# A graph convolution on one core: first nodes loaded in two parts, the last group but one multiplied tile by tile, the last group scaled from PSUM

## The chip, the cores and the metric

The kernel runs on one core of one Trainium2 chip. Its metric is the device time of one execution in microseconds; several executions are timed, and the median is compared. The core's engines are TensorE (PE in the profile, with its weight loads as PEld), VectorE (DVE), ScalarE (ACT), GpSimd (POOL) and SyncE (SP), which only issues DMAs here.

## The reference

One equivariant graph convolution with a residual and a layer norm over 12,500 nodes of 128 features and 412,500 edges, which come sorted by destination node:

```python
f0 = x0 @ W1_0e / sqrt(32);  f1 = einsum('nui,uw->nwi', x1, W1_1o) / sqrt(32)
feat, self = halves of f0, f1
h   = gelu(gelu(edge_attr_8 @ W_mlp1 / sqrt(8)) @ W_mlp2 / sqrt(64))
w00, w01, w10, w11 = h @ Wp_00, h @ Wp_01, h @ Wp_10, h @ Wp_11      # per edge
e0, e1 = feat0[src], feat1[src];  ea0, ea1 = edge_attr_4[:, :1], edge_attr_4[:, 1:]
mid0 = concat(w00*e0*ea0, w11*sum(e1*ea1)/sqrt(3))
mid1 = concat(w01*e0*ea1, w10*e1*ea0)
n0, n1 = segment_sum(mid0, dst), segment_sum(mid1, dst)
y = cos(pi/8)*self + sin(pi/8)*(n0 @ W2_0e, einsum(n1, W2_1o))
out = layernorm(x + y)            # over the 128 features of a node
```

## The kernel before

**Tiling.** Nodes go in 25 groups of 512 (four tiles of 128; the last group, 24, has one full tile and one of 84). Edges go in 806 runs of 512 (four tiles of 128), four runs to a chunk, 202 chunks. Destination nodes are sorted, so a chunk's edges reach a window of at most 96 nodes from the chunk's first node (`first_at`), and each tile's edges a narrower window from the tile's own first node (`tile_first`, shown as `tf` in the profile).

**First stage.** For each group, PE transposes the loaded rows of `x` (`turn`, L294), ACT copies them to `xT` (L295), PE multiplies by the weights (`features_of`, L301), DVE copies the product (L304) and ACT's queue stores it to a DRAM table (`store_nodes`, L260). SP's queue loads `x` six groups ahead (L252), one small load a group from the list of `weight_loads` (L925), the edge inputs of the first chunks (`load_edges`, L496), and after the groups the addresses for the main loop (`aid_load`, `aid_at` and `pick` in the profile, L959). POOL gathers rows of `x` for the first 18 runs with indirect DMAs (`gather`, L222).

**Main loop, one run at a time.** POOL gathers from the table, 18 runs ahead, into one of 19 buffers `G`. A few of a run's rows are not gathered: DVE (L190) and ACT (L192) pick columns out of `xT`, which PE multiplies (L198), and SP copies some rows singly (L209). PE and ACT compute the edge weights (`radial`, `mlp1` L536 and L540, `mlp2` L551 and L556, `weights` L569), DVE forms the messages `M` (L637, L641), PE sums them into the chunk's window (`segments`, L666 and L668; L660 clears the window), and DVE adds the window to the accumulator (`add`, L681). Before it builds a chunk's selection, DVE reads one element of each of its gathered tiles (`seen`, L597), which waits for those gathers.

**Node groups.** When a group's edges are all in (`due`), `norm` calls `moments`: PE multiplies each of its tiles by `ws` (L698) and by four blocks of `wpost` (L701) into a PSUM tile named `h`, which has two buffers that the edge weights use too; ACT copies the result to `y` (L706, L708). `statistics` (DVE, L714, L715), `deviations` (L720, L721) and `normalise` (L727 to L742) follow a chunk later, and SP stores the group. Group 23 (`before_last`) is multiplied in run 801 (chunk 200), group 24 in `norm_last` after the last run.

**Order.** Each engine's order is the order of the code. DMAs of SP's and ACT's queues share eight completion counters (`DMAHW0` to `DMAHW7`), handed out in turn; a DMA is not issued before the one that had its counter last has landed, whichever of the two queues issued that.

Of the kernel before, what the change touches and what calls it, by code (L numbers as in the profile page):

```python
# [53 lines left out]
LNB = 2  # L54
TURN_AT = (7, 9, 11, 13, 15, 17, 18, 20, 22, 24)
# [3 lines left out]
def gnn_kernel(ctx: ExitStack, tc: tile.TileContext, x, src, dst, ea4, ea8, w1_0, w1_1, wm1, wm2,  # L59
# [277 lines left out]
    def weight_loads():  # L337

        yield w1r, sub(wm1, 0, [[0, P // RAD], [HID, RAD], [1, HID]])
        yield w2b, sub(wm2, 0, [[0, 2], [HID, HID], [1, HID]])  # L340
        for j, w in enumerate((wp00, wp01, wp10, wp11)):
            yield wpb[:, j * MUL:(j + 1) * MUL], sub(w, 0, [[0, 2], [MUL, HID], [1, MUL]])
        for t, w in ((w20, w2_0), (w21, w2_1)):
            yield t[:MUL, :], w[:MUL, :]
            yield t[MUL:, :], sub(w, MUL * MUL, [[0, 3], [MUL, MUL], [1, MUL]])
        yield first_node, sub(dst, 0, [[1, 1], [CH * SB, NCH]])
        for b, t in enumerate(tile_first):
            c0, n = b * P, t.shape[0]
            last = c0 + n == NCH and E < NCH * CH * SB
            if last:  # L350
                yield (t[n - 1:n, :].rearrange("a (k o) -> a k o", o=1),
                       sub(dst, (NCH - 1) * CH * SB, [[1, 1], [0, CH * Q], [1, 1]]))
                k = -(-(E - (NCH - 1) * CH * SB) // P)
                yield t[n - 1:n, :k], sub(dst, (NCH - 1) * CH * SB, [[k * P, 1], [P, k]])
            yield t[:n - last], sub(dst, c0 * CH * SB, [[CH * SB, n - last], [P, CH * Q]])
# [52 lines left out]
    def tile_places():  # L408

        for b, t in enumerate(tile_first):  # L410
# [8 lines left out]
            nc.vector.tensor_scalar(t, off, 4.0, None, op0=OP.mult)  # L419
# [225 lines left out]
    def places(c):  # L645

        b, r = divmod(c, P)
# [37 lines left out]
    before_last = due[NCH - 1][0] - 1  # L685

    def moments(b, sums=None):
        n0, nn, full, tail, tiles = group(b)
        if not pend:
# [3 lines left out]
        j = len(pend)  # L693
        pend.append(b)
        pt = ps.tile([P, XB, P], F32, name="h")
        at = n0 - base[-1] if b in due[NCH - 1] else 0
        for t, k in tiles:
# [5 lines left out]
            else:  # L703
                nc.vector.tensor_tensor(pt[:k, t, :], pt[:k, t, :], sums[:k, t, :], op=OP.add)
        if full:
            nc.scalar.activation(Y["y"][:, j, :full, :], pt[:, :full, :], AF.Copy)  # L706
        if tail:
            nc.scalar.activation(Y["y"][:tail, j, full, :], pt[:tail, full, :], AF.Copy)  # L708

    def statistics(b):  # L710
        j = pend.index(b)
        st = wk.tile([P, XB, 6], F32, name="bst")
        for t, k in group(b)[4]:
            nc.vector.bn_stats(st[:k, t, :], Y["y"][:k, j, t, :])  # L714
# [8 lines left out]
    def normalise(last=False, keep=False):  # L723
# [9 lines left out]
        for j, b in enumerate(pend):  # L733
            if b in done:
                continue
            for t, k in group(b)[4]:
                i = j * XB + t - i0
                if last and t % 2:
                    nc.vector.tensor_scalar(y[:k, j, t, :], y[:k, j, t, :], r[:k, i:i + 1], m[:k, i:i + 1],
                                            op0=OP.mult, op1=OP.add)  # L740
                    continue
                nc.scalar.activation(y[:k, j, t, :], y[:k, j, t, :], AF.Identity,  # L742
                                     bias=m[:k, i:i + 1], scale=r[:k, i:i + 1])
            store_nodes(nc.sync, out, b, y[:, j])
# [4 lines left out]
    def norm(bs):  # L749
        for b in bs:  # L750
            moments(b)
# [14 lines left out]
    def norm_last(bs):  # L766
# [6 lines left out]
        if len(pend) > len(done):  # L773
            deviations()
            normalise(True)

# [119 lines left out]
    with tc.manual_schedule(engines={PE, ACT, DVE, SP}):  # L896
# [7 lines left out]
        for b in range(min(AHEAD, NG)):  # L904
# [9 lines left out]
                 NG // 2 + 9: tile_places, NG // 2 + 10: lambda: mlp2(1), NG // 2 + 11: make_ws, NG: make_wpost}  # L914
# [20 lines left out]
        late = list(aid_load())  # L935
# [10 lines left out]
        for s in range(NCH * CH + CH):  # L946
# [79 lines left out]
            if s == 2:  # L1026
                nc.vector.memset(owns[1], 0.0)
            if s == 5:
# [38 lines left out]
```

## Time and profile before

| | |
|---|---|
| median of 3 runs | 3556.44 us (3555.64 to 3560.35) |
| the profiled execution: its time, its span | 3556.29 us, 3554.4 us |
| PE, PEld busy | 3159.9 us (89%), 2755.6 us (78%) |
| DVE busy | 3129.2 us (88%) |
| ACT busy | 2797.6 us (79%) |
| POOL busy | 2667.6 us (75%) |
| mean granted clock of PE | 0.932 |

In rows of instructions the columns are the start in us from the span's start, the duration in us, engine, line, operation, output and inputs, count, and in brackets the idle time of the engine before it with what ended it. Rows that say SPq or ACTq are issues of DMAs. In rows of waits they are the time in total, the number, and the longest. In rows of windows they are the stretch, its length, the busy time of PE, PEld, DVE, ACT and POOL with their instructions, the granted clock, the busy share of the DMA engines and GB/s. In rows of groups they are the count, the busy time with the mean of one in ns, and the idle time before them. In rows of one tile's instructions they are the count, the shortest, median and longest duration in ns, and when the first and the last start. Rows of the chain are its pieces in order of time: start, length, what ran.

### The profile page before, as it was taken

What the parts mean: (1) busy time and instruction counts of PE and PEld (TensorE: products, weight loads), DVE (VectorE), ACT (ScalarE), POOL (GpSimd) and SP (SyncE); (2) the same over time, 40 slices, a digit from 0 to 9 for tenths busy, and PEclk for the clock granted to TensorE, in tenths of its full rate; (3) what the DMA queues carried; (4) which work ended last, traced back from release to release, by engine and by line L of the source; (5) the groups of instructions that cost most, each with busy time, mean ns of one, the idle gap of its engine ahead of it and who ended that gap; (6) DMA issues with size and microseconds to landing.
All of it is one profiled execution on the core that took longest, in us unless ns stands there. A gap on an engine that the chain in (4) does not pass through costs nothing. (4 is left out here: it accounts for less than half of the span.)

```text
span 3554.4 us, 143693 instructions
## 1 busy us (share of the span) xinstructions
PE 3159.9 (89%) x28598; PEld 2755.6 (78%) x28598; DVE 3129.2 (88%) x29317; ACT 2797.6 (79%) x23671; POOL 2667.6 (75%) x2804
## 2 busy tenths in 40 slices
PE   6899898998898988998899898898899989888888
PEld 6777777787777777877788787787787777777777
DVE  2699999999999999999899899888899888889897
ACT  3488788788888888887887888877787887788785
POOL 7777777777777777777777777777777777777775
PEclk8999999998999999899998899989899999999998
DMA  8322332223322223322323323323323232232221
GB/s 199 70 62 68 63 64 65 63 61 74 64 60 67 63 60 74 64 60 62 68 61 70 67 59 64 65 63 68 65 62 64 59 69 63 60 69 63 60 65 47
DMA packets 579225, 239.29 MB, mean 67 GB/s; under 512 B 483651, under 2 KB 528747, under 8 KB 578347
## 3 DMA queue, kind: packets, MB, share of 16 engines
q0 software_dynamic: 89536, 183.55, 20.3%
q1 hardware_dynamic: 468041, 40.02, 9.1%
q10 hardware_dynamic: 20770, 6.47, 0.8%
q8 instruction: 252, 4.13, 0.5%
q14 instruction: 626, 5.13, 0.5%
HBM read 217.00 MB, written 12.80 MB: 65 GB/s over the span
## 5 line engine op out<-in xcount | busy, mean ns | idle before, releaser
L222 POOL DMA_INDIRECT G<-table,idx x2726 | 2598.9, 953 | 836.7 <-issue 718.5
L192 ACT ACTIVATE gt<-xT 128x1 f32 x22016 | 2166.7, 190 | 73.3 <-issue 53.6
L190 DVE COPY gt<-xT 128x1 f32 x25216 | 1728.6, 144 | 212.1 <-issue 172.9
L666 PE MATMUL sums<-own,M 128*128 128x96 f32 x6446 | 1354.8, 294 | 74.3 <-DVE M L641 73.0
L668 PE MATMUL sums<-own,M 128*128 128x96 f32 x6446 | 1319.7, 288 | 85.1 <-DVE M L641 84.1
L666 PEld LDWEIGHTS sums<-own,M 128*128 128x128 f32 x6446 | 1037.5, 201 | 181.9 <-DVE M L641 101.7
L668 PEld LDWEIGHTS sums<-own,M 128*128 128x128 f32 x6446 | 1035.3, 202 | 108.9 <-DVE M L641 107.6
L641 DVE TENSOR_TENSOR M<-w,G 128x384 f32<-128x384 f32 x1612 | 880.1, 547 | 0.0
L569 PE MATMUL w<-wpb,h 64*128 64x128 f32 x6448 | 649.3, 305 | 57.8 <-DVE M L641 56.3
L569 PEld LDWEIGHTS w<-wpb,h 64*128 64x128 f32 x6448 | 496.5, 197 | 199.6 <-issue 74.3
L637 DVE TENSOR_TENSOR M<-w,G 128x256 f32<-128x256 f32 x806 | 333.4, 414 | 34.4 <-issue 19.9
L540 ACT ACTIVATE h<-h 128x512 f32<-128x512 f32 x404 | 216.3, 586 | 178.6 <-PE h L536 165.7
L536 PE MATMUL h<-eT,w1b 64*128 64x128 f32 x3232 | 288.7, 319 | 8.4 <-ACT e L523 8.3
L536 PEld LDWEIGHTS h<-eT,w1b 64*128 64x128 f32 x3232 | 241.3, 218 | 38.7 <-ACT e L523 13.7
L556 ACT ACTIVATE h<-h 128x512 f32<-128x512 f32 x404 | 213.5, 577 | 26.3 <-PE h L551 22.5
L551 PE MATMUL h<-h,w2b 64*64 64x256 f32 x3232 | 222.6, 391 | 0.0
L199 ACT ACTIVATE G<-h 128x128 f32<-128x128 f32 x369 | 96.4, 277 | 120.5 <-PE h L198 76.4
L198 PE MATMUL h<-wf,gt 128*128 128x128 f32 x738 | 143.5, 294 | 1.9 <-ACT h L556 0.9
L529 ACT ACTIVATE eT<-h 128x128 f32<-128x128 f32 x202 | 56.0, 277 | 112.7 <-PE h L527 89.5
L551 PEld LDWEIGHTS h<-h,w2b 64*64 64x64 f32 x3232 | 104.5, 133 | 44.8 <-issue 0.5
L630 DVE TENSOR_TENSOR own<-oh,e 128x512 f32<-128x512 f32 x202 | 137.6, 681 | 0.7 <-issue 0.2
L681 DVE TENSOR_TENSOR acc<-sums,acc 128x384 f32 x202 | 111.2, 550 | 9.7 <-issue 6.2
(113 smaller groups left out, 1329.1 us busy)
## 6 DMA issues: line engine op xcount, KB each, us to landing
G<-table SPq DMA_DIRECT2D x7168, 0.5 KB
G<-table,idx POOLq DMA_INDIRECT x2726
e<-in_edge_attr SPq DMA_DIRECT2D x201, 64.0 KB
own<-in_x SPq DMA_DIRECT2D x24, 256.0 KB
table<-acc ACTq DMA_DIRECT2D x24, 256.0 KB
xt<-in_edge_attr SPq DMA_DIRECT2D x24, 256.0 KB
out<-y SPq DMA_DIRECT2D x24, 256.0 KB
xt<-in_dst SPq DMA_DIRECT2D x5, 256.0 KB
```

The costliest lines, as they stand in the source:

```text
L190: nc.vector.tensor_copy(to, col)
L192: nc.scalar.activation(to, col, AF.Copy)
L222: nc.gpsimd.indirect_dma_start(out=G[s][:, q, :], out_offset=None, in_=x if s < raw_runs else table, in_offset=bass.IndirectOffsetOnAxis(a ...
L536: nc.tensor.matmul(p1[h][:, j // 2, j % 2, :], w1b[rows, j, :], eT[c][rows, :], start=True, stop=True)
L540: nc.scalar.activation(H1[c][h], p1[h].rearrange("p k j e -> p (k j e)"), AF.Gelu_apprx_tanh, scale=1.0 / math.sqrt(RAD))
L551: nc.tensor.matmul(p2[r][k * HID:(k + 1) * HID, h * n:(h + 1) * n], w2b[rows, :], H1[c][h][rows, k * n:(k + 1) * n], start=True, stop=True)
L556: nc.scalar.activation(H2[c][r].rearrange("p k j e -> p (k j e)"), p2[r], AF.Gelu_apprx_tanh, scale=1.0 / math.sqrt(HID))
L569: nc.tensor.matmul(WP[i][:, q, :], H2[c][q % 2][rows, k, q // 2, :], wpb[rows, :], start=True, stop=True)
L637: nc.vector.tensor_tensor(M[s][:, :, :, :MUL], w[:, :, :2 * MUL].rearrange("p q (a u) -> p q a u", a=2), g[:, :, None, :MUL].to_broadcast( ...
L641: nc.vector.tensor_tensor(M[s][:, :, j, MUL:].rearrange("p q (i u) -> p q i u", i=3), w[:, :, None, (2 + j) * MUL:(3 + j) * MUL].to_broadc ...
L666: nc.tensor.matmul(flat[:, bass.ds(at, 4 * FIRST_HALF)].bitcast(F32), M[s][:, q, 0, :], own[:, 3 * WIDE:], start=False, stop=False)
L668: nc.tensor.matmul(sb[:, 1:, bass.ds(at, 4 * WIDE)].bitcast(F32), M[s][:, q, 1, :], own[:, :3 * WIDE].rearrange("p (a j) -> p a j", a=3), ...
```

## The change

**First nodes in two parts.** `tile_first` is cut into three tiles (of 16, 128 and 58 chunks) instead of two (128 and 74). The first is loaded ahead of the weights, the other two after the main loop's addresses (`late`), and DVE turns them into places in run 9 instead of in the first stage. Each element is a 4-byte piece of its own, so such a load has 16 pieces a chunk. The load of the chunks' first nodes (`first_node`) stays in the list of weights.

**Last group but one by tiles.** `done_at` gives the chunk with which each of group 23's four tiles has its last edge: 193, 195, 197, 199. After chunks 193, 195 and 197 `moments` multiplies one tile (in runs 779, 787 and 795) and ACT copies it; in run 801 only the fourth is left. `find_first` raises the first nodes of the chunks between, so that no window reaches into a tile that has been multiplied.

**Last group from PSUM.** Group 24 is not copied to `y`: its statistics and its scaling read the PSUM tile, and its two tiles are stored one by one, one from ACT's queue and one from SP's.

```diff
 def weight_loads():
+    yield from tile_loads(0)
     yield w1r, ...
     ...
     yield first_node, sub(dst, 0, [[1, 1], [CH * SB, NCH]])
-    for b, t in enumerate(tile_first): ...           # the loads of both tiles
+def tile_loads(b):                                   # the same loads, of one tile
+    t, c0 = tile_first[b], tile_from[b]
...
-NT = -(-NCH // P)
-tile_first = [cst.tile([min(P, NCH - b * P), CH * Q], I32, name=f"tf{b}") for b in range(NT)]
+tile_from = [0, *range(FIRST_TILES, NCH, P)]         # FIRST_TILES = 16
+NT = len(tile_from)
+tile_first = [cst.tile([z - a, CH * Q], I32, name=f"tf{b}")
+              for b, (a, z) in enumerate(zip(tile_from, tile_from[1:] + [NCH]))]
+before_last = due[NCH - 1][0] - 1
+done_at = [math.ceil((before_last * GN + (t + 1) * P + MARGIN) / N * NCH) - 1 for t in range(XB)]
 def find_first():
+    for t, (a, z) in enumerate(zip(done_at, done_at[1:])):
+        nc.vector.tensor_scalar(strays[:, a + 1:z + 1], strays[:, a + 1:z + 1], float((t + 1) * P), None, op0=OP.max)
-def moments(b, sums=None):
+def moments(b, sums=None, part=None):
+    if part is not None:
+        tiles = tiles[part:part + 1]
...
+    if sums is None and b == NG - 1:
+        Y["pt"] = pt
+        return
+    if part is not None:
+        nc.scalar.activation(Y["y"][:, j, part, :], pt[:, part, :], AF.Copy)
+        return
+def rows_of(b, j, t, k):
+    return Y["pt"][:k, t, :] if b == NG - 1 and "pt" in Y else Y["y"][:k, j, t, :]
 def statistics(b):
-        nc.vector.bn_stats(st[:k, t, :], Y["y"][:k, j, t, :])
+        nc.vector.bn_stats(st[:k, t, :], rows_of(b, j, t, k))
 def normalise(last=False, keep=False):               # scales rows_of(...) into y, and:
+                if last:
+                    eng = nc.sync if t % 2 else nc.scalar
+                    eng.dma_start(out[b * GN + t * P:b * GN + t * P + k, :], y[:k, j, t, :])
-            store_nodes(nc.sync, out, b, y[:, j])
+            if not last:
+                store_nodes(nc.sync, out, b, y[:, j])
 def norm(bs):
-            moments(b)
+            moments(b, part=XB - 1 if b == before_last else None)
...
-        late = list(aid_load())
+        late = list(aid_load()) + [load for b in range(1, NT) for load in tile_loads(b)]
+            if k == 3 and c - 1 in done_at[:-1]:
+                moments(before_last, part=done_at.index(c - 1))
+            if s == 9:
+                tile_places(range(1, NT))
```

**What it moves on SP.** In the first stage, from the last load of `x` to the loads of addresses, SP's queue had before (`own1` holds `x`, `tf1` is the tile of 74 chunks, `e8` the edge inputs of chunk 3):

```order
L254 DMA own1_75<-in_x 84x128 [waits DMAHW0_49,PE_49]
L925 DMA tf1_95<-in_dst 1x7x1 [waits DMAHW6_49,DMAHW2_49]
L925 DMA tf1_95<-in_dst 73x16x1 [waits DMAHW3_49]
L496 DMA e8_828<-in_edge_attr_8 128x16x8 [waits DMAHW4_49]
L959 DMA aid_at_68<-in_src 56x128 [waits DMAHW5_49]
L959 DMA pick0_830<-in_src 128x128
L959 DMA pick128_831<-in_src 69x128 [waits DMAHW7_49]
L959 DMA pick197_832<-in_src 19x128 [waits DMAHW1_49]
L959 DMA pick197_832<-in_src 19x128 [waits DMAHW2_49]
```

and has now:

```order
L255 DMA own1_75<-in_x 84x128 [waits DMAHW7_49,PE_49]
L512 DMA e8_819<-in_edge_attr_8 128x16x8 [waits DMAHW1_49]
L993 DMA aid_at_68<-in_src 56x128 [waits DMAHW2_49]
L993 DMA pick0_821<-in_src 128x128 [waits DMAHW3_49]
L993 DMA pick128_822<-in_src 69x128 [waits DMAHW4_49]
L993 DMA pick197_823<-in_src 19x128 [waits DMAHW5_49]
L993 DMA pick197_823<-in_src 19x128 [waits DMAHW6_49]
L993 DMA pick197_823<-in_src 18x128 [waits DMAHW0_49]
L993 DMA pick197_823<-in_src 18x128 [waits DMAHW1_49]
```

The load of 73 x 16 pieces is gone from ahead of the edge inputs; ten picks later, behind the last of them, come the loads of the 128 and of the 57 x 16 pieces.

**What it moves on ACT.** The stores of groups 17 and 18 to the table, with what stands between them, before:

```order
L260 DMA table_78<-acc_207 128x4x128 [waits DMAHW0_49,DVE_49]
L556 ACTIVATE h20_652<-h_642 128x512 [waits PE_49]
L556 ACTIVATE h21_654<-h_643 128x512 [waits PE_49]
L588 ACTIVATE G_136<-h_656 128x512 [waits DMASW2_49,DMASW1_49,DMASW3_49,DMASW0_49,PE_49]
L295 ACTIVATE xT_66<-w_662 128x512 [waits PE_49]
L260 DMA table_78<-acc_207 128x4x128 [waits DMAHW2_49,DVE_49]
```

The second of them is counted by `DMAHW2`, and so waits for SP's fifth DMA behind the edge inputs, the second one of 19 rows. Now:

```order
L261 DMA table_78<-acc_208 128x4x128 [waits DMAHW7_49,DVE_49]
L572 ACTIVATE h20_650<-h_640 128x512 [waits PE_49]
L572 ACTIVATE h21_652<-h_641 128x512 [waits PE_49]
L604 ACTIVATE G_137<-h_654 128x512 [waits DMASW2_49,DMASW1_49,DMASW3_49,DMASW0_49,PE_49]
L296 ACTIVATE xT_66<-w_660 128x512 [waits PE_49]
L261 DMA table_78<-acc_208 128x4x128 [waits DMAHW1_49,DVE_49]
```

It is counted by `DMAHW1` and waits for SP's seventh DMA behind the edge inputs. The first of the two waits for the last load of `x`, before and now.

**What it moves on DVE.** At the very end DVE's order now is (`h` is the PSUM tile of group 24):

```order
L743 BN_AGGR mv_199341<-bst_204218 128x2 [waits DVE_49]
L742 BN_STATS bst_204218<-h_204207 84x6
L743 BN_AGGR mv_199341<-bst_204218 84x2 [waits DVE_49]
L748 TENSOR_SCALAR rs_204223<-mv_199341 128x4 [waits DVE_49]
L755 RECIPROCAL rs_204223<-rs_204223 128x4 [waits Activation_49]
L757 TENSOR_TENSOR rs_204223<-rs_204223 128x4 [waits DVE_49]
L758 SCALAR_TENSOR_TENSOR rs_204223<-rs_204223 128x4 [waits DVE_49]
L759 SCALAR_TENSOR_TENSOR rs_204223<-rs_204223 128x4 [waits DVE_49]
L760 SCALAR_TENSOR_TENSOR rs_204223<-mv_199341,rs_204223 128x4 [waits DVE_49]
L768 TENSOR_SCALAR y_199340<-h_204207,rs_204223 84x128 [waits Activation_49]
```

The statistics wait for PE alone, where before they waited for ACT's copy. The last instruction, the scaling of the 84 nodes, waited for DVE's own results before and now waits for ACT, which scales the other tile out of the same PSUM tile.

More of the change, by code (lines that the diff above doesn't have):

```diff
@@ L346, in weight_loads @@
         yield first_node, sub(dst, 0, [[1, 1], [CH * SB, NCH]])
[L347 to L355, printed above, removed]
+    def tile_loads(b):
+        t, c0 = tile_first[b], tile_from[b]
+        n = t.shape[0]
+        last = c0 + n == NCH and E < NCH * CH * SB
+        if last:
+            yield (t[n - 1:n, :].rearrange("a (k o) -> a k o", o=1),
+                   sub(dst, (NCH - 1) * CH * SB, [[1, 1], [0, CH * Q], [1, 1]]))
+            k = -(-(E - (NCH - 1) * CH * SB) // P)
+            yield t[n - 1:n, :k], sub(dst, (NCH - 1) * CH * SB, [[k * P, 1], [P, k]])
+        yield t[:n - last], sub(dst, c0 * CH * SB, [[CH * SB, n - last], [P, CH * Q]])
     def make_w1b():
@@ L392, in gnn_kernel @@
     first_at = cst.tile([1, NCH], I32)
-    NT = -(-NCH // P)
-    tile_first = [cst.tile([min(P, NCH - b * P), CH * Q], I32, name=f"tf{b}") for b in range(NT)]
+    tile_from = [0, *range(FIRST_TILES, NCH, P)]
[3 more added lines that the diff above has]
+    before_last = due[NCH - 1][0] - 1
+    assert len(due[NCH - 1]) == 1
+    done_at = [math.ceil((before_last * GN + (t + 1) * P + MARGIN) / N * NCH) - 1 for t in range(XB)]
+    assert due[done_at[-1]] == [before_last] and done_at == sorted(set(done_at))
+    assert not any(c in due for c in range(done_at[0] - 1, done_at[-1])) and done_at[-1] < NCH - 2
     def find_first():
@@ L645, in places @@
     def places(c):
[L647 removed]
+        b = max(b for b, a in enumerate(tile_from) if a <= c)
+        r = c - tile_from[b]
         _, PLACE[c] = nc.values_load_multi_w_load_instructions(
@@ L692, in moments @@
             nc.vector.memset(Y["v"], 1.0)
-        j = len(pend)
-        pend.append(b)
+        if b not in pend:
+            pend.append(b)
+        j = pend.index(b)
         pt = ps.tile([P, XB, P], F32, name="h")
```

20 lines of the change are left out of this document (12 added, 8 removed).

## The prediction

> **What bounds the kernel now.** I read the page's groups first, then POOL's instructions in order of time, then DVE's waits and the chain that ended last, and then the two ends of the kernel. The costliest group:
>
> ```profile
> span 3554.4 us, 143693 instructions
> L222 POOL DMA_INDIRECT G<-table,idx x2726 | 2598.9, 953 | 836.7 <-issue 718.5
> ```
>
> 2598.9 us of work and 836.7 us of gaps make 3435.6 us for 2726 gathers: POOL has nothing but gathers for nearly the whole span, 1.26 us each. In order of time:
>
> ```profile
> 3.84 1.09 POOL L222 DMA_INDIRECT G<-in_x,idx_raw  x1 [2.67 <-DMA idx_raw<-in_src]
> ...
> 92.74 0.94 POOL L222 DMA_INDIRECT G<-in_x,idx_raw  x1 [0.30 <-issue]
> 99.37 0.94 POOL L222 DMA_INDIRECT G<-table,idx  x1 [5.68 <-DVE M L641]
> ...
> 3528.32 0.94 POOL L222 DMA_INDIRECT G<-table,idx  x1 [0.30 <-issue]
> ```
>
> The 72 gathers from `x` take 1.25 us each without a break. From the first gather from the table to the last lie 3428.95 us and 2725 steps, 1.258 us each: at 1.25 us a step, some 20 us of waiting in all. The one large gap is 5.68 us, before the first gather from the table, which needs the whole table in DRAM. DVE, who uses the rows:
>
> ```profile
> 98.40 0.42 DVE L637 TENSOR_TENSOR M<-w,G 128x256 f32<-128x256 f32 x1
> ...
> 3471.61 0.37 DVE L597 COPY SEEN<-G 128x4 f32<-128x4 f32 x2 [1.32 <-DMA G<-table,idx]
> ```
>
> ```profile
> DVE SEEN L597 <- DMA G<-table,idx: 36.8, 32, 2.1
> ```
>
> ```profile
> 3467.72 0.94 POOL G L222
> 3468.97 2.49 DMA G<-table,idx
> ```
>
> At 98.40 POOL has gathered the first 18 runs and DVE has used none. Late in the kernel DVE waits for gathers, and the chain that ended last still passes through POOL's gather at 3468.97. So DVE eats up POOL's lead, and POOL's pace sets the time up to here. Two rules follow. A microsecond that only DVE, ACT or PE gains early is lost again in a wait for gathers; a microsecond by which POOL's first gather from the table comes earlier is kept. And behind 3471 the end counts directly.
>
> **The start: loads moved.** Why the table is late is on SP's and ACT's queues:
>
> ```profile
> 62.43 0.41 SPq L254 DMA_DIRECT2D own<-in_x  x1
> 65.16 1.58 SPq L925 DMA_DIRECT2D tf<-in_dst  x2
> 66.80 8.94 SPq L496 DMA_DIRECT2D e<-in_edge_attr  x1
> ...
> 76.87 11.40 SPq L959 DMA_DIRECT2D pick<-in_src  x16
> 88.32 0.46 SPq L496 DMA_DIRECT2D e<-in_edge_attr  x1
> ```
>
> ```profile
> 71.02 0.60 ACT L295 ACTIVATE xT<-w 128x512 f32<-128x512 f32 x1 [0.26 <-PE w L294]
> 81.27 0.38 ACTq L260 DMA_DIRECT2D table<-acc  x1
> 81.75 1.08 ACT L540 ACTIVATE h<-h 128x512 f32<-128x512 f32 x2 [10.13 <-DMA pick<-in_src]
> ...
> 97.05 0.62 ACTq L262 DMA_DIRECT2D table<-acc  x1
> ```
>
> The same issue of edge inputs takes SP 0.46 us alone and 8.94 us right behind the two pieces of `tf`. Meanwhile ACT, done at 71.62, stands before a store whose counter was last given to a pick, and all that ACT and PE do next stands with it: 10.13 us. The fourth pick's issue ends at about 79.7 (76.87 + 4 x 0.71), and the store goes 1.5 us later.
>
> In the changed order nothing of `tf` stands ahead of these edge inputs, but ACT's store now waits for the sixth pick. From 62.84, where the last load of `x` is issued: edge inputs 1 us, addresses 1 us, six picks at 0.71 us, then 1.5 us make 70.6, against ACT's 71.62. So the wait goes, and with it some 10 us of the first stage; what comes next is POOL's own work, which ends its last gather from `x` at 93.68. Today 2.3 us pass from the last store's issue to the gather. For a gather at 93.98 that store must be issued by 91.7, 5.4 us earlier than 97.05, of 10 to be had. The gain for POOL is the gap down to its usual 0.30: 5.4 us. It cannot be more.
>
> That the 73-chunk load is to blame is read from its place alone, and so I leave a rival in which it is not (the failed start, below) a chance of 0.15. The Trainium skill ("DMA: Bandwidth & Descriptors", on why a DMA increments its semaphore by 16) has a load run on as many DMA engines as the largest number up to 16 that divides its outermost sizes. By that rule 73 chunks go through one engine, 1168 pieces in a row, and 57 through three; the sum would be the same and the rival nearly without a chance. No row here shows the load of 57.
>
> That load and the one of 128 chunks now lie on SP behind the picks, with the edge inputs of chunk 4 behind them. The stores of groups 22 and 24 take over their counters, so a late load would hold the table. By the sums above they are issued near 75 to 80, and their stores are due no earlier than 82; I count nothing. DVE's new work in the loop is twelve instructions on `tf` in run 9 and three in run 1, against six taken out of the first stage:
>
> ```profile
> L419 DVE TENSOR_SCALAR tf<-off x2: 180/184/188, 87.8 to 89.0; 128x16 int32<-128x16 f32 x1, 74x16 int32<-74x16 f32 x1
> ```
>
> Fifteen at 0.2 us make 3 us, at a place where DVE has a lead of 18 gathered runs; nothing. Without that cover they would cost the 3 us.
>
> **The multiplying by tiles.** PE at the end, DVE behind it, and what PE meets at the new places:
>
> ```profile
> 3474.97 0.46 PE L666 MATMUL sums<-own,M 128*128 128x96 f32 x2 [1.97 <-DVE M L641]
> ...
> 3508.36 0.72 PE L569 MATMUL w<-wpb,h 64*128 64x128 f32 x8
> ...
> 3527.97 0.41 PE L698 MATMUL h<-ws,xT 128*128 128x128 f32 x2
> ...
> 3531.35 0.39 PE L698 MATMUL h<-ws,xT 128*128 128x128 f32 x2
> ...
> 3536.21 0.42 DVE L637 TENSOR_TENSOR M<-w,G 128x256 f32<-128x256 f32 x1 [5.08 <-PE w L569]
> ```
>
> ```profile
> PEld h L698 <- ACT h L556: 49.6, 23, 3.2
> ```
>
> In run 801 three tiles take 3.38 us (3527.97 to 3531.35), and DVE stands for PE's weights: all that PE does next comes 3.4 us earlier. The cost: each of three earlier parts takes 1.13 us, and at such a place PE first waits for ACT to free the PSUM tile, 49.6 / 23 = 2.2 us; 3.3 us a part. The one in run 779 lies some 40 us ahead of PE's idle 1.97 us at 3474.97, so PE has made up for it by then. The one in run 787 lies right ahead of that idle time; 2.0 of its 3.3 us vanish there, the rest in the waits of the next chunks. The one in run 795 goes ahead of 3508.36. Whether it is hidden depends on the clock:
>
> ```profile
> 3470.00:3480.00 10.00, 7.31 (x46) 6.51 (x46) 8.00 (x81) 4.80 (x43) 7.54 (x8) 0.78 0.22 55
> 3480.00:3490.00 10.00, 10.00 (x56) 8.82 (x55) 8.54 (x80) 6.27 (x51) 7.67 (x8) 0.50 0.38 66
> 3500.00:3510.00 10.00, 10.00 (x109) 8.82 (x108) 9.38 (x94) 9.39 (x90) 7.56 (x9) 1.00 0.21 54
> ```
>
> ```profile
> 3525.87 0.30 PEld L666 LDWEIGHTS sums<-own,M 128*128 128x128 f32 x2 [0.45 <-DVE M L641]
> ```
>
> Here the clock fell to 0.50 right after that idle time, PE fell behind and had no free time in 3500 to 3510; only at 3525.87 does it wait for DVE again, 0.45 us. In this state the part of run 795 costs 3.3 - 0.5 = 2.8 us and the gain is 0.6. Without a fall of the clock in the last 60 us it is hidden and the gain is 3.4. I take 3.4, because the part of run 787 fills the idle time ahead of the fall, and keep 0.6 as the other end.
>
> The Trainium skill ("TensorE: Matmul & The Clock Gate", Part 1) has the clock halved after an idle window of about 3.4 us; the rows fit in so far as the fall follows the idle time. By that rule the change keeps the clock up here and the sum is the one with 3.4.
>
> **The end.**
>
> ```profile
> 3545.09 1.04 PE L701 MATMUL h<-wpost,acc 128*84 128x128 f32 x8
> 3546.28 0.26 ACT L706 ACTIVATE y<-h 128x128 f32<-128x128 f32 x1
> 3546.57 0.29 DVE L714 BATCH_NORM_STATS2 bst<-y 128x6 f32<-128x128 f32 x1 [1.94 <-ACT y L706]
> 3548.93 0.34 DVE L739 TENSOR_SCALAR y<-y,rs 84x128 f32<-84x128 f32 x1
> 3548.99 0.49 ACT L742 ACTIVATE y<-y,rs 128x128 f32<-128x128 f32 x1 [1.09 <-DVE rs L732]
> 3549.97 0.72 SPq L262 DMA_DIRECT2D out<-y  x1
> ```
>
> The statistics can start when PE ends, at 3546.13, and not at 3546.57: 0.4 us. The two scalings now follow one another, since DVE waits for ACT: DVE's 0.34 us ends at about 3549.9 of the old clock, where the second store was issued anyway, at 3549.97. Each queue has one store. So 0.4 us is left; between 0 and 0.7 us.
>
> **Sum.** 5.4 + 3.4 + 0.4 = 9.2 us. The profiled execution took 3556.29 us, 1.9 us more than its span and 0.15 us less than the median of the three runs (3556.44), so 3547.1 us. A measurement of this kernel can tell about 0.2%, 7.1 us, from no change.
>
> **Rivals.**
>
> The clock falls late: as in this trace, PE is behind in run 795, and the gain there is 0.6 instead of 3.4. 3556.3 - 5.4 - 0.6 - 0.4 = 3549.9 us. For it: the trace has just this; against it: the idle time before the fall is filled.
>
> The change doesn't do what it says at the start: the 8.94 us come from the loads of `x` in the queue, not from `tf`. Then the sixth pick ends eight later, the store goes at 78.6 instead of 81.27, and POOL gains 2.7 instead of 5.4; with a late load of `tf` holding the last stores, none. 3549.8 to 3552.5 with the full gain at the end, 3555.3 with the small one and no gain at the start. Against it: 0.46 us for the same issue elsewhere.
>
> Slower: PE becomes the bound from run 779 on. It decides if the three parts find no idle time of PE, and each waits as long as the longest of its kind, 3.2 us: 3 x (3.2 + 1.13) = 13.0 us on the path, against 3.4 + 5.4 + 0.4 saved. 3560.1 us. From 9.2 us on the change is a loss. Against it: PE's idle 1.97 us at 3474.97 shows slack after the second part.
>
> **How the numbers follow.** The forecast has 0.48, the late fall 0.30, the failed start 0.15, slower 0.07. The range takes in the forecast with 0.7 instead of 0.4 at the end and the scatter of the runs downward (0.8 us): 3545.7, rounded to 3545.5; upward the late fall and the failed start up to 3553.0. The bound of 7.1 us below the median is 3549.3: the forecast's own runs pass it mostly (0.42 of 0.48), the late fall, 0.6 us short of it, in under half (0.13), the failed start rarely (0.02): faster 0.57. Same 0.36, slower 0.07.
>
> **What would show it.** Right: the first gather from the table 0.3 us behind the last one from `x`; ACT's wait of 10 us at the store gone; the last gather near 3523; DVE's wait of 5.08 us in run 804 down to under 2; the last statistics right behind PE. The prediction is wrong if the gap at the table stays, if POOL's step grows beyond 1.258 us, or if PE has no idle time between runs 779 and 800.

## The result, and the profile after

| | before | after |
|---|---|---|
| median of 6 runs | 3556.04 us (3551.65 to 3560.35) | 3544.68 us (3543.31 to 3548.95) |
| the profiled execution: time, span | 3556.29 us, 3554.4 us | 3543.32 us, 3541.5 us |
| ratio of the times, 95% interval | | 0.9971 [0.9959, 0.9983] |
| mean granted clock of PE | 0.932 | 0.933 |

The changed kernel is faster by 11.4 us in the medians (6.0 to 14.6 us by the interval), and by 12.9 us in the two profiled spans. The line numbers of the rows below are those of the changed kernel: gathers L223, edge inputs L512, addresses L993, stores to the table L261 and L263, group nodes by tiles L717 and L720, messages L653 and L657, weights L585.

**POOL.** The page's group of gathers, then POOL's instructions in order of time:

```profile
L223 POOL DMA_INDIRECT G<-table,idx x2726 | 2595.3, 952 | 831.5 <-issue 706.8
```

```profile
92.86 0.94 POOL L223 DMA_INDIRECT G<-in_x,idx_raw  x1 [0.31 <-DVE acc L420]
94.11 0.95 POOL L223 DMA_INDIRECT G<-table,idx  x1 [0.30 <-DVE M L657]
...
3519.57 0.94 POOL L223 DMA_INDIRECT G<-table,idx  x1 [0.30 <-issue]
```

The gap of 5.68 us in front of the first gather from the table is 0.30 us now, and that gather starts at 94.11 instead of 99.37: 5.26 us. The last gather starts at 3519.57 instead of 3528.32: 8.75 us. So the 2725 steps between them take 3425.46 us instead of 3428.95, 3.49 us less. From the last gather to the end it is 21.9 us instead of 26.1: 4.2 us. 5.26 + 3.49 + 4.2 make the 12.9 us of the spans.

**The start.** SP's issues, then ACT's instructions around the store of group 18 and the last stores to the table:

```profile
62.99 0.38 SPq L512 DMA_DIRECT2D e<-in_edge_attr  x1
...
65.53 11.53 SPq L993 DMA_DIRECT2D pick<-in_src  x16
77.10 6.04 SPq L993 DMA_DIRECT2D tf<-in_dst  x4
83.19 2.77 SPq L512 DMA_DIRECT2D e<-in_edge_attr  x1
```

```profile
71.05 0.38 ACTq L261 DMA_DIRECT2D table<-acc  x1
71.53 1.08 ACT L556 ACTIVATE h<-h 128x512 f32<-128x512 f32 x2 [1.45 <-PE h L552]
...
86.34 0.64 ACTq L263 DMA_DIRECT2D table<-acc  x1
```

The edge inputs take SP 0.38 us where they took 8.94. ACT issues the store of group 18 at 71.05 instead of 81.27. What ACT does next waits for PE, not for a pick; but it was close: the sixth pick landed at 70.97, and DVE's copy, which the store sends, ended at 71.02. The last store goes at 86.34 instead of 97.05. The 57 x 16 pieces of the last load of first nodes hold the next edge inputs for 2.77 us, and no store waits for them.

**The end.** DVE's first messages, those of run 788 and those of run 800; then, of the kernel before, those of runs 788 and 800 and PE's first product of group 24:

```profile
87.90 0.42 DVE L653 TENSOR_TENSOR M<-w,G 128x256 f32<-128x256 f32 x1
...
3465.77 0.41 DVE L653 TENSOR_TENSOR M<-w,G 128x256 f32<-128x256 f32 x1
...
3515.66 0.42 DVE L653 TENSOR_TENSOR M<-w,G 128x256 f32<-128x256 f32 x1
```

```profile
3474.04 0.42 DVE L637 TENSOR_TENSOR M<-w,G 128x256 f32<-128x256 f32 x1
...
3524.93 0.41 DVE L637 TENSOR_TENSOR M<-w,G 128x256 f32<-128x256 f32 x1
```

```profile
3543.00 0.41 PE L698 MATMUL h<-ws,xT 128*128 128x128 f32 x2
```

The changed kernel's PE at two of the earlier parts and in run 801, DVE in run 804, and the last group:

```profile
3465.62 0.49 PE L717 MATMUL h<-ws,xT 128*128 128x128 f32 x2 [2.63 <-ACT h L572]
...
3496.48 0.49 PE L717 MATMUL h<-ws,xT 128*128 128x128 f32 x2 [2.44 <-ACT h L572]
...
3518.70 0.41 PE L717 MATMUL h<-ws,xT 128*128 128x128 f32 x2
...
3523.59 0.42 DVE L653 TENSOR_TENSOR M<-w,G 128x256 f32<-128x256 f32 x1 [1.74 <-PE w L585]
...
3530.38 0.41 PE L717 MATMUL h<-ws,xT 128*128 128x128 f32 x2
...
3532.47 1.04 PE L720 MATMUL h<-wpost,acc 128*84 128x128 f32 x8
...
3533.55 0.30 DVE L742 BATCH_NORM_STATS2 bst<-h 128x6 f32<-128x128 f32 x1 [1.53 <-PE h L720]
...
3536.85 0.36 SPq L775 DMA_DIRECT2D out<-y  x1
```

DVE's wait in run 804 is 1.74 us instead of 5.08, and the last statistics follow PE's end (3533.51) by 0.04 us. The clock, in two stretches of 20 us that begin just ahead of those two parts:

```profile
3460.00:3480.00 20.00, 17.10 (x168) 15.14 (x168) 18.09 (x176) 16.56 (x148) 15.12 (x17) 1.00 0.30 61
3490.00:3510.00 20.00, 17.50 (x173) 15.42 (x172) 17.62 (x179) 14.59 (x130) 15.12 (x17) 1.00 0.23 56
```

It does not fall in them, where before it was 0.50 in the ten microseconds from 3480. Behind the first part, in run 779, it is at half for one step of 3.4 us, from 3434.0.

**Other chips.** The pair above ran on one chip. The experiments ran on five others, on which the kernel before takes 5529 to 5592 us, so their times are compared only with runs of their own chip, and their traces are read stage by stage. In one of these runs (e9) the profiled execution was a disturbed one, 4068.9 us at a clock of 0.647, and is not read.

### The profile page after: what moved, and what is told of

Same layout as the page of the kernel before. It is cut to its first block, busy times and chain, and to the rows that moved or that the text cites. A ratio compares the mean times of both kernels' runs of the same rounds, so it can differ in the third digit from the quotient of the medians.

```text
span 3541.5 us, 143700 instructions
## 1 busy us (share of the span) xinstructions
PE 3151.0 (89%) x28598; PEld 2747.1 (78%) x28598; DVE 3132.4 (88%) x29326; ACT 2797.2 (79%) x23672; POOL 2664.1 (75%) x2804
## 5 line engine op out<-in xcount | busy, mean ns | idle before, releaser
L223 POOL DMA_INDIRECT G<-table,idx x2726 | 2595.3, 952 | 831.5 <-issue 706.8
L657 DVE TENSOR_TENSOR M<-w,G 128x384 f32<-128x384 f32 x1612 | 881.3, 548 | 0.0
L585 PE MATMUL w<-wpb,h 64*128 64x128 f32 x6448 | 647.2, 305 | 55.7 <-DVE M L657 55.4
L585 PEld LDWEIGHTS w<-wpb,h 64*128 64x128 f32 x6448 | 495.6, 198 | 195.3 <-DVE M L657 71.9
L653 DVE TENSOR_TENSOR M<-w,G 128x256 f32<-128x256 f32 x806 | 334.0, 414 | 29.6 <-issue 16.2
```

What stands on the lines that cost most here:

```text
L223: nc.gpsimd.indirect_dma_start(out=G[s][:, q, :], out_offset=None, in_=x if s < raw_runs else table, in_offset=bass.IndirectOffsetOnAxis(a ...
L585: nc.tensor.matmul(WP[i][:, q, :], H2[c][q % 2][rows, k, q // 2, :], wpb[rows, :], start=True, stop=True)
L653: nc.vector.tensor_tensor(M[s][:, :, :, :MUL], w[:, :, :2 * MUL].rearrange("p q (a u) -> p q a u", a=2), g[:, :, None, :MUL].to_broadcast( ...
L657: nc.vector.tensor_tensor(M[s][:, :, j, MUL:].rearrange("p q (i u) -> p q i u", i=3), w[:, :, None, (2 + j) * MUL:(3 + j) * MUL].to_broadc ...
```

## What is different on the other chips

The windows of the stretch in which POOL gathers from `x`, of the changed kernel on the first chip and then of e4, the same kernel on another chip:

```profile
20.00:90.00 70.00, 55.84 (x471) 50.92 (x470) 26.06 (x61) 28.74 (x53) 53.06 (x56) 0.92 0.88 220
```

```profile
20.00:90.00 70.00, 5.86 (x24) 5.05 (x24) 1.38 (x2) 1.19 (x2) 52.95 (x56) 0.52 0.33 86
```

POOL does the same 56 gathers in the same time. PE does 471 instructions beside them on the first chip and 24 on the other, DVE 61 and 2. On the other chips a gather nearly stops the other engines; where POOL has none, they run as on the first chip. Two things follow. The first stage is not covered by POOL there, so that all of what the loads are worth shows in when the table is ready. And from run 788 on, where POOL has done all its gathers, one sees what PE, ACT and DVE need by themselves. Why a gather stops the others there, and not on the first chip, no run shows.

## Experiments

**e1 and e10, the loads alone** (e10 is the same kernel on another chip). The kernel before, with the three tiles of first nodes and this alone:

```diff
+        yield from tile_loads(0)
...
-        late = list(aid_load())
+        late = list(aid_load()) + [load for b in range(1, NT) for load in tile_loads(b)]
...
+            if s == 9:
+                tile_places(range(1, NT))
```

> The kernel before with the first nodes' loads of the change alone (three tiles, two of them behind the picks, places in run 9); groups 23 and 24 as before. Theory of the prediction: the first gather from the table comes 0.30 us behind the last one from x, 5.4 us earlier, and all of it is kept: 5.4 us less than the kernel before (about 3550.7 against 3556.1), and from the last gather to the end 26 us as before. Rival, lost in the loop: the gather starts 5.4 us earlier but DVE's waits for gathers or POOL's slow gathers take it back: 0 to 2 us less. Rival, steps of POOL: the two loads also make the loop itself shorter, the 2725 steps take about 3425.5 us instead of 3429, and the kernel is about 9 us faster.

> The kernel before with the loads of the change alone, as in the first study, with all gathers. On a chip like the first one (kernel before near 3556 us): theory 5.4 us less, the first gather from the table 0.30 us behind the last from x, all of it kept; rival 0 to 2 us, lost again in the loop. On a chip like the second one (near 5530 to 5590 us): ACT's wait for a pick at the store of group 18 gone again, the first gather from the table some 10 us earlier than in the kernel before, and 5 to 13 us less time.

e1: 5583.66 us against 5592.13, ratio 0.9991 [0.9977, 1.0005]; e10: 5528.58 against 5536.25, 0.9989 [0.9976, 1.0002]. Each interval just includes no change. SP's and POOL's rows in e1:

```profile
135.79 0.39 SPq L505 DMA_DIRECT2D e<-in_edge_attr  x1
...
149.68 5.89 SPq L969 DMA_DIRECT2D tf<-in_dst  x4
155.61 2.50 SPq L505 DMA_DIRECT2D e<-in_edge_attr  x1
```

```profile
161.78 0.94 POOL L223 DMA_INDIRECT G<-table,idx  x1 [68.27 <-DVE M L650]
```

To compare with them stands e2, below, whose first stage is that of the kernel before: the first gather from the table starts at 161.78 here and at 172.90 there, 11 us later (in e3, which has the same first stage as e2, at 171.81). In e10 it starts at 161.86. The size of the stall is as predicted ("some 10 us of the first stage"); how much of it counts depends on what covers it, 5.26 us on the first chip.

**e2, the multiplying by tiles alone.** The kernel before, with `done_at`, the clamp in `find_first`, the `part` of `moments` and this:

```diff
+            if k == 3 and c - 1 in done_at[:-1]:
+                moments(before_last, part=done_at.index(c - 1))
...
-            moments(b)
+            moments(b, part=XB - 1 if b == before_last else None)
```

> The kernel before with group 23 multiplied tile by tile alone (first nodes' loads and group 24 as before). Theory: first gather from the table as before behind a gap of 5.7 us, and from the last gather to the end 26.1 - 3.4 = 22.7 us; 3.4 us less than before (about 3552.7). Rival, late fall of the clock: 0.6 us less. Rival, parts not hidden: PE is behind from run 779, up to 13 us on the path, same or slower. Rival, steps of POOL: the loop from the first to the last gather from the table is itself some 3.5 us shorter than 3429, then about 7 us less in all.

5598.56 us, ratio 1.0009 [0.9995, 1.0022]. SP, ACT and POOL in the first stage, and PE at the part of run 795:

```profile
138.84 1.58 SPq L938 DMA_DIRECT2D tf<-in_dst  x2
140.48 7.98 SPq L504 DMA_DIRECT2D e<-in_edge_attr  x1
```

```profile
154.26 1.09 ACT L548 ACTIVATE h<-h 128x512 f32<-128x512 f32 x2 [8.75 <-DMA pick<-in_src]
```

```profile
172.90 0.94 POOL L222 DMA_INDIRECT G<-table,idx  x1 [79.49 <-DVE M L649]
```

```profile
5547.77 0.80 PE L708 MATMUL h<-ws,xT 128*128 128x128 f32 x2 [2.44 <-ACT h L564]
```

From the messages of run 788 to the end it takes 81.5 us; the kernels without the parts (e1, e3, e5, e10) take 78.0 to 78.9. So in this execution the parts cost more than they bring, by some 3 us. The clock is at half until 5516.4, from a fall at 5506.2, ahead of run 788, and for 10.2 us behind the part of run 795. Neither the 3.4 nor the 0.6 us of the two expectations came, nor the 13.

**e3, the last group from PSUM alone.** `rows_of`, `Y["pt"]` and the two stores of `normalise`, as in the change's diff.

> The kernel before with group 24 read from PSUM and stored tile by tile alone. Theory: the last statistics start when PE ends, 0.4 us less (0 to 0.7), not to be told from the scatter of the times, but to be read from the trace: 6.8 us from the end of the last sums to the last store's issue become 6.4. Rival: the tail is shorter by more, since with two stores of one tile each the end of the kernel behind the last store changes too: up to 1 us.

0.9998 [0.9985, 1.0011]. From the messages of run 788 to the end 78.0 us, against 78.4 in e1. The 0.4 us between these two can't be told from scatter, since e6 has 78.0 without this edit; but from the end of the last sums to the last store's issue it takes 6.31 us here and 6.80 in the kernel before and in e1. So it is 0.5 us where 0.4 were expected, and nothing more.

**e4, the whole change** on the chip of e1 to e3, no edit.

> The changed kernel as it is, once more, for its scatter. Theory: of the 12.8 us between the two profiled spans, 5.3 are the start and 4.2 the end, and the other 3.5 us are a scatter of POOL's gathers between executions: this profile has a loop of 3425 to 3430 us from the first to the last gather from the table, and the five runs together lie 9 to 10 us below the kernel before. Rival: the change shortens the loop itself: 3425.5 us again, and runs 12 to 13 us below.

5588.56 us, 0.9997 [0.9984, 1.001]. On these chips the whole change makes no measurable difference, and neither do its parts: 0.9 per mille less with the loads and 0.9 more with the tiles, each the middle of an interval that includes none. The question about the loop on the first chip could not be answered here. PE at the parts of runs 787 and 795, and the clock behind them:

```profile
5509.44 0.49 PE L717 MATMUL h<-ws,xT 128*128 128x128 f32 x2 [2.84 <-ACT h L572]
...
5543.41 0.49 PE L717 MATMUL h<-ws,xT 128*128 128x128 f32 x2 [2.45 <-ACT h L572]
```

```profile
5505.00:5525.00 20.00, 16.89 (x137) 14.54 (x135) 15.25 (x149) 13.81 (x122) 0.00 (x0) 0.83 0.09 7
5540.00:5560.00 20.00, 17.55 (x150) 15.57 (x148) 15.21 (x149) 11.82 (x101) 0.00 (x0) 0.83 0.01 3
```

PE waits as in the changed kernel on the first chip (2.63 and 2.44 us), but here each wait is followed by 6.8 us of half clock (a mean of 0.83 over 20 us). Run 788 to the end: 81.8 us.

**e5, the load of 73 chunks made one of 80.** The kernel before, no load moved:

```diff
-    tile_first = [cst.tile([min(P, NCH - b * P), CH * Q], I32, name=f"tf{b}") for b in range(NT)]
+    tile_from = [0, 121]                             # tiles of 121 and 81 chunks instead of 128 and 74
```

> The kernel before, its two tiles of first nodes cut at chunk 121 instead of 128, and nothing else: the second load becomes 80 x 16 pieces (more bytes than 73 x 16), at the same place ahead of the edge inputs; the first 121 x 16. Theory (a load of 73 chunks runs on one DMA engine and blocks SP's queue): the issue of the edge inputs behind it falls from 8.94 us to about 0.5, ACT's wait before the store of group 18 from 10.1 to about 1 us, the first gather from the table comes 0.3 us behind the last one from x, and the kernel is 5.4 us faster than before, without any load being moved. Rival (the queue is full of loads of x, whatever stands behind them): the issue takes 8 to 9 us as before, the gap at the table stays 5.7 us, same time.

5589.51 us against 5591.9, 0.9989 [0.9973, 1.0006]: no measurable change of the time.

```profile
140.48 1.47 SPq L929 DMA_DIRECT2D tf<-in_dst  x2
142.01 1.22 SPq L499 DMA_DIRECT2D e<-in_edge_attr  x1
```

```profile
149.56 1.08 ACT L543 ACTIVATE h<-h 128x512 f32<-128x512 f32 x2 [3.04 <-DMA pick<-in_src]
```

```profile
166.97 0.95 POOL L222 DMA_INDIRECT G<-table,idx  x1 [73.45 <-DVE M L644]
```

More bytes at the same place, and SP is held for 1.22 us instead of 7.98; ACT's wait is 3.04 us instead of 8.75, and the table comes 5.9 us earlier than in e2 and 4.8 earlier than in e3, which are on another chip. The queue full of loads of `x` is the same in both, so the rival falls: the number of chunks in the load was to blame. ACT's wait stays 2 us longer than expected, since in this order the store still waits for a pick behind the load. The rule of the Trainium skill ("DMA: Bandwidth & Descriptors", on why a DMA increments its semaphore by 16: as many engines as the largest number up to 16 that divides the outermost size) gives 1 engine for 73 chunks, 3 for 57 and 16 for 80; the next issue took 7.98, 2.50 and 1.22 us, in that order.

**e6 and e7, without gathers from the table**, before and after the change. POOL clears the same rows instead, so their messages are zero:

```diff
+            if s >= raw_runs:
+                nc.gpsimd.memset(G[s][:, q, :], 0.0)
+                continue
```

> The kernel before with its 2726 gathers from the table left out (POOL clears the same rows instead, so their messages are zero); all else as before, the 72 gathers from x too. It measures what the other engines need by themselves. On the chip of the last five runs the kernel before takes 5592 us, and the engines stand still in most of the time in which POOL gathers. Theory (there a gather keeps the other engines from going on; on the first chip POOL's pace is the bound and the others are faster): without gathers the last 12 runs before run 800 took 4.07 us each on that chip, 806 runs some 3290 us, and with the start about 3450 us. Rival (that chip gives out instructions slowly, whatever POOL does): it stays above 5000 us. Rival of the prediction's first step (PE or DVE is the bound and POOL only follows): about 3550 us on any chip.

> The changed kernel with the same gathers left out. With no gather to wait for, PE has no slack at the end, and every part of the change shows at its own price. Theory: table 10 us earlier (the start is not covered by POOL's gathers here on the second chip), two to three parts by tiles at 2 to 3.3 us each, 3.3 us back in run 802, 0.4 us at the end: 4 to 10 us less than the same kernel before the change. Rival (parts are free wherever they stand): 13.7 us less. Rival (parts and the clock behind them cost more than they bring): less than 4 us, or more time than before.

e6 takes 3554.94 us where the kernel with gathers takes 5532.26 on that chip: the rival of a chip that gives out instructions slowly falls. My 3450 us were too low, and the number is that of the other rival, in which PE or DVE is the bound. But it comes about by the slow start: the first messages start at 172.4 here (98.40 on the first chip), and from there to the end it takes 3384 us. With POOL on the first chip it takes 3456 us (98.40 to 3554.4), 72 us more. So PE and DVE alone are not the bound there, but by 2% only, as far as two chips can be compared.

e7 takes 3544.43 us (3535.95 to 3553.16), 10.5 us less than e6 (3547.35 to 3558.43); these are four runs each, and they overlap. Between the two profiled spans lie 10.3 us. The loads bring 9.9 us of them (first messages at 162.5), and the end takes 2.6 back: from run 788 on it takes 78.0 us in e6 and 80.6 in e7. The other 2.9 us lie in the loop between, where two kernels as alike as e11 and e12 below differ by 9 us.

**e8, the early parts three runs later.** The changed kernel, with the part multiplied behind the sums of a run in which no weights' tile of PSUM is in use:

```diff
+            if k == 2 and c - 2 in done_at[:-1]:     # right behind segments(s - 1)
+                moments(before_last, part=done_at.index(c - 2))
-            if k == 3 and c - 1 in done_at[:-1]:
-                moments(before_last, part=done_at.index(c - 1))
```

> The changed kernel with the three early parts of group 23 three runs later (behind the sums of runs 781, 789 and 797, and not behind the multiplication whose PSUM tile PE then waits for). Theory: the price of a part is 1.13 us of work and 2.4 to 2.8 us of waiting for ACT to free the PSUM tile, and on the second chip the clock falls behind each wait. Without the wait the time from the messages of run 788 to the end of the kernel falls from 81.7 us in the changed kernel to 74 to 77 us, below the 78.4 us of the kernel before; no fall of the clock right behind the parts. Rival (the falls of the clock have nothing to do with the waits): 76 to 79 us, with the falls still there. Rival (PE waits for ACT at the new place as well): 81 us again.

5525.81 us against 5532.26, 1.0001 [0.9986, 1.0017]. Run 788 to the end: 78.1 us. PE does not wait at the parts:

```profile
5452.13 0.41 PE L717 MATMUL h<-ws,xT 128*128 128x128 f32 x2
...
5485.25 0.41 PE L717 MATMUL h<-ws,xT 128*128 128x128 f32 x2
```

That is 3.7 us better than e4, less than the theory, and within the first rival's bounds. In this run the clock stood at half until 5442, from POOL's last gathers, so that run 788 began behind, and it fell once more for 3.4 us at 5479.9, between the two parts and behind neither. This left open how much is the wait and how much the clock. e9, e11 and e12 leave the gathers out.

**e9, e11 and e12, the same without gathers.** e9 and e12 are e8 with the edit of e6, e11 is e7 again.

> The changed kernel without its gathers from the table, and with the early parts of group 23 three runs later (both edits as in the last two studies). Measured so far without gathers: from the messages of run 788 to the end 78.0 us for the kernel before, 80.6 us for the changed one, whose parts wait 1.5 to 2.8 us for ACT and are followed by falls of the clock. Theory (a part costs its 1.13 us, the rest is the wait and the clock): 80.6 less 2.8 and 2.1 us of waits and about 2 us of half clock, 74 to 76 us, and a kernel 4 to 6 us below the changed one without gathers (3544 us). Rival (a part delays DVE by its whole 3.3 us wherever it stands): 80 us.

> The changed kernel without its gathers from the table, once more, beside the next run on the same chip. From the messages of run 788 to the end 80.6 us as before, with falls of the clock behind the parts; 3544 us.

> The same with the early parts three runs later, so that PE does not wait for ACT to free the PSUM tile. Theory: 74 to 77 us from the messages of run 788 to the end, no idle time of PE over 1 us in front of a part and no fall of the clock behind it, 3 to 6 us less than the run beside it. Rival (a part costs DVE its 3.3 us wherever it stands): 80 to 81 us and the same time.

e9's four other runs took 3532.0 to 3544.1 us, with no run to compare on that chip. e11 took 3544.07 us and e12 3543.69 us, on one chip: no difference in time, where 3 to 6 us were expected. In the traces there is one. For e7, e11 and e12, in this order: DVE's messages of run 788, then the windows of 20 us around the two parts.

```profile
3465.85 0.42 DVE L656 TENSOR_TENSOR M<-w,G 128x256 f32<-128x256 f32 x1
```

```profile
3460.00:3480.00 20.00, 16.90 (x137) 14.80 (x137) 16.40 (x159) 13.52 (x117) 0.00 (x0) 0.83 0.08 8
3490.00:3510.00 20.00, 17.68 (x148) 15.70 (x147) 17.19 (x171) 14.53 (x132) 0.00 (x0) 0.83 0.01 2
```

```profile
3466.14 0.41 DVE L656 TENSOR_TENSOR M<-w,G 128x256 f32<-128x256 f32 x1
```

```profile
3460.00:3480.00 20.00, 16.90 (x150) 14.72 (x148) 17.75 (x172) 14.76 (x130) 0.00 (x0) 0.91 0.09 9
3490.00:3510.00 20.00, 17.68 (x182) 15.77 (x182) 18.58 (x183) 17.14 (x147) 0.00 (x0) 1.00 0.01 2
```

```profile
3454.14 0.41 DVE L656 TENSOR_TENSOR M<-w,G 128x256 f32<-128x256 f32 x1
```

```profile
3455.00:3475.00 20.00, 18.19 (x170) 15.85 (x172) 18.39 (x187) 16.50 (x149) 0.00 (x0) 1.00 0.09 8
3485.00:3505.00 20.00, 18.44 (x174) 15.75 (x174) 18.23 (x168) 10.34 (x67) 0.00 (x0) 1.00 0.01 2
```

PE at the second part, of e7 and then of e11:

```profile
3500.22 0.49 PE L720 MATMUL h<-ws,xT 128*128 128x128 f32 x2 [2.32 <-ACT h L575]
```

```profile
3498.92 0.38 PE L720 MATMUL h<-ws,xT 128*128 128x128 f32 x1 [2.32 <-ACT h L575]
```

e7 and e11 are the same kernel, with the same waits of PE (2.83 and 2.32 us). In e7 the clock is at half for 6.8 us behind each, in e11 for 3.4 us behind the first and not at all behind the second.

| run 788 to the end | parts wait | at half clock behind them | us |
|---|---|---|---|
| e6, no early parts | | none | 78.0 |
| e7 | 2.83 and 2.32 | 13.6 us | 80.6 |
| e11 | 2.83 and 2.32 | 3.4 us | 75.6 |
| e12 | no | none | 74.6 |

At half clock PE loses half the time: 6.8 us in e7, 1.7 in e11. The difference of 5.1 us is what the two measured, 5.0. Without it e7 and e11 would take 73.8 us, e12 74.6, and e6 less the gains of run 802 and of the end (3.3 and 0.4) 74.3. So both the work of the parts and the wait ahead of them are hidden to within 1 us, even without POOL's gathers. What they cost is the fall of the clock where one follows the wait. I had expected the wait to cost its 2.8 and 2.1 us; by this sum it costs nothing by itself. That e12's span is 13 us shorter than e11's is no merit of the edit: 12 us of them are there at run 788, ahead of which the two differ only in the first part.

## Why the prediction was right, and where not

**Direction and size.** Right: forecast 3547.1 us, measured 3544.68. Against the kernel before in the same runs that is 0.9971, which makes 3546.1 us of the 3556.44 that the prediction starts from. But the median itself lies 0.8 us below the low end of the range. That end was sized too narrowly: it took 0.8 us for "the scatter of the runs downward", from three runs, where six runs of the kernel before spread over 8.7 us. Its sum is wrong too: 3547.1 less 0.3 less 0.8 is 3546.0 and not 3545.7.

**POOL's pace, and what is kept.** Borne out. The first messages start at 87.90 instead of 98.40, 10.5 us earlier, but POOL's first gather from the table only 5.26, and in run 788 DVE is 8.3 us ahead (3465.77 against 3474.04): what DVE gained beyond POOL was lost again. The pace itself was taken as equal, and here 3.49 us more came than the sum had; so the last gather came at 3519.57, where 3523 was named as the sign. They lie in the gathers' own time, 2595.3 instead of 2598.9 us; their idle time without the gap at the table is 831.2 us after and 831.0 before. More closely, they lie in a few slow gathers: before, 104 of the 2726 took over 1 us, together 25.6 us beyond 0.95 each, and after it 86, together 21.6 us. So the "20 us of waiting" of the prediction were slow gathers and not waits. The change does not touch the gathers, and runs of one kernel differ by more than this. On the chip of e1 to e4 it goes the other way: the gathers of the whole change (e4) took 2583.0 us, those of its parts 2577.6 to 2578.8. That speaks for scatter, but no run on the first chip tests it. The 3.49 us are most of the difference between the 9.2 us of the sum and the 12.9 of the spans. The medians' 11.4 us and their interval hold the 9.2.

**The start, 5.4 us.** 5.26 us. The cause is shown by e5, if on another chip, and on the first chip the same issue took 0.38 us once the load was gone; the failed start, which had 0.15, is excluded. That the stores behind 82 would not be held by the late loads was right too.

**The multiplying by tiles, 3.4 us.** From the messages of run 800 to the first matrix product of group 24 it takes 14.72 us (3515.66 to 3530.38) instead of 18.07 (3524.93 to 3543.00): 3.35 us. The waits of 2.63 and 2.44 us were near those of the row that was used (2.2). That the early parts are hidden was right by e11 and e12. On the first chip it is less sharp: from run 788 to run 800, with two parts of 7.3 us in all, it takes 49.89 us after and 50.89 before, where the clock was at half for 20.5 us; e1, e5 and e6, without parts and without a fall there, take 48.4 to 48.9. So 1 to 1.5 us of the 7.3 may be on the path there, or DVE waits that long for gathers; no run separates the two.

The reason given for the clock was wrong. I wrote that "the part of run 787 fills the idle time ahead of the fall". The part itself has PE idle for 2.6 us in front of it, and in e4 and e7 a fall follows such a wait. What decided is how the wait lies across the clock's steps of 3.41 us (see below). In the changed kernel on the first chip the two waits lay across a border, with 1.69 and 0.94 us of PE's idle time in one step and the next, and 1.36 and 1.08, and no fall followed; in e11 the second wait was parted the same way, 1.18 and 1.13. In e7 2.59 and 2.32 us lay in a single step, in e4 2.24 and 2.08, in e11's first part 2.83, and each was followed by a fall (in e2 so was a wait of 2.44 us with 1.79 in one step). That the clock stayed up there was thus luck. So "late fall" deserved more than 0.30, and its price was too small: with two falls the change loses 2.6 us at the end without gathers (e7 against e6) instead of gaining 0.6.

The kernel before on the first chip was at half clock for 20.5 us from 3475.7; run 788 to the end took 80.4 us there, and 78.0 in e6, which has neither that fall nor the gathers.

**The end, 0.4 us.** From the first matrix product of group 24 to the end 11.1 us (3530.38 to 3541.5) instead of 11.4 (3543.00 to 3554.4): 0.3. From the end of the last sums to the last store's issue it is 6.3 us instead of 6.8, as in e3.

**Slower, PE the bound from run 779 on.** It did not come, and it needed its three waits on the path; without gathers, where PE has least slack, the waits were hidden. The longer end on the other chips (e2, e4) goes with another mechanism, the falls of the clock.

## What to carry to other kernels

Look at what a queue's slow issue stands behind: a load of 73 x 16 small pieces held SP for 8.94 us, and through a completion counter ACT for 10, where on another chip one of 80 x 16 held SP for 1.22. Count a gain on an engine that another paces only as far as the pacing engine moves. And where work is put in front of a wait of PE, the wait may cost nothing and still bring the clock down behind it: put it where the PSUM tile is free. In e12 that kept the clock up, though the times of e11 and e12 do not differ.

## What the runs showed of the hardware

**The clock.** It changes in steps of 3.41 us, at half or at full. Counted over the whole trace by the gaps in PE's records, a step with at least 1.1 us idle stands ahead of 70 of the 72 falls in the kernel before, and of all 74 in the changed one; of the steps at full clock without a fall behind them 30 of 824 and 36 of 822 have so much. From 1.7 us on, half a step, a fall is nearly sure: it followed 40 of 44 such steps before and 39 of 41 after. Between 1.1 and 1.7 us it followed 30 of 56 and 35 of 69. The Trainium skill ("TensorE: Matmul & The Clock Gate", Part 1) speaks of an idle window of about 3.4 us, which would make waits of 2.3 to 2.8 us harmless; here half a window was enough, and a wait counts by how it lies across two of them. The fall at 3475.7 in the kernel before, too, followed a step with 2.2 us idle, so that the prediction's reading of it by that rule does not hold.

**Gathers and the other engines.** On five of six chips PE, ACT and DVE came nearly to a stand beside POOL's gathers: in the 70 us of the windows above PE did 24 to 36 instructions there instead of 471, and SP issued 6 DMAs in e4 instead of 56. The kernel took 5529 to 5592 us there instead of 3556; without gathers 3555. The 56 gathers of these windows took POOL 53 us in both.
